# Sums of the attention weights on VectorE for some groups, and other durations in the order's account

## The chip, the cores and the metric

The kernel runs on one core of a Trainium2 chip. The metric is the device time of one execution in microseconds (us), as the median of several runs; a shorter time is better. The engines of the core are TensorE (PE), VectorE (DVE), ScalarE (ACT), GpSimd (POOL) and SyncE (SP), which issues most DMAs.

## The reference

One transformer block with adaptive layer norm, in float32, on `x` of 8 x 1024 x 512, with 16 heads of 32 and a hidden width of 2048:

```python
mod = jax.nn.silu(condition) @ Wada + bada
sh_a, sc_a, gt_a, sh_m, sc_m, gt_m = jnp.split(mod, 6, axis=1)
xm = _layernorm(x, g1, be1) * (1.0 + sc_a[:, None, :]) + sh_a[:, None, :]
x = x + gt_a[:, None, :] * _attention(xm, Wqkv, Wproj, bproj)      # causal softmax
xm = _layernorm(x, g2, be2) * (1.0 + sc_m[:, None, :]) + sh_m[:, None, :]
x = x + gt_m[:, None, :] * (jax.nn.gelu(xm @ W1 + b1, approximate=False) @ W2 + b2)
```

## The kernel before, in words

**Tiling.** The 8 sequences are cut into 16 blocks of 512 tokens: `blocks[n]` is a sequence and its half h. The 16 heads form four groups g of four heads (`HPG = 4`), each with 32 of 128 partitions. The linear parts (`k`, `q`, `v`, `u`, `proj`, `d`) are products of 128x32 weight columns, four side by side in PE's array; most are done by a Strassen scheme (`strassen`, `down`). `matmul` (line 212) issues the four column tiles; in float32 each shows up as two records.

**Attention.** For each group, `scores_at_once` fills the one score tile (`st`, four banks of PSUM) with scores by query, and DVE takes their row maxima (lines 1607 and 1610). `weights_T` fills the same tile with scores by key minus the maxima; ACT takes the exponential into a slot in SBUF (`pT`, line 1698). There are three slots, in `free_p`. POOL masks the diagonal (line 1703). `weigh` multiplies the weights with V into `po`, and `add_weights` lets POOL add every further unit's weights to those of the group's first unit (line 1816), whose slot is the sum, `acc`. The small last unit of groups 0 and 2 is shared with the following group, and its slot is held until both have used it.

**The end of a group** (`finish`, line 1736). Four matmuls with a 128x32 tile of ones add `acc` over its 128 keys and spread the sum over the 32 partitions of each head (line 1747, column-tiled). After them the slot is free. ACT copies the sums into `rec` (line 1756) and `po` into `top` (line 1759); DVE inverts `rec` in four pieces of 128 columns (line 1765); POOL multiplies the two into `qT` (line 1790), which `proj` reads later. Once the end of group 3 is done, `written["attended", n]` lets `proj` of block n go.

**The order.** The program of each engine is written in the order in which Python emits it. An account, `now`, keeps a time for each engine, and `note`, `note_pe` and `note_act` add a duration for each instruction and keep the times at which results are ready (`written`) and buffers free (`left`). PE's part of the account adds `SWITCH` when the tiling changes between "rows" (scores) and "columns" (the rest). Decisions are taken from the account: which thread of linear work goes next (`work`), how much of it is put ahead of an attention unit (`step_aside`), whether a copy goes to DVE or ACT (`sooner`), an addition to DVE or POOL (`either`), or a combination to DVE alone or to an ACT copy and an addition (`combine_out`). Work off PE waits in `jobs`; `run_jobs` emits the head of that list once its operands are due, and `run_jobs(True)` emits all of it.

Of the kernel before, what the change touches and what calls it, by code (L numbers as in the profile page):

```python
# [22 lines left out]
def kernel(  # L23
# [112 lines left out]
    def note_pe(ns, form, reads=(), writes=()):  # L136
        now["PE"] = max(now["PE"], due(reads, writes))
        if shape[0] != form:
            shape[0] = form
            now["PE"] += SWITCH  # L140
        note("PE", ns, reads)
        spent[0] += ns
        for k in writes:
            written[k] = now["PE"] + PIPE
# [14 lines left out]
    def either(out, a, b, op, reads, writes):  # L159

        n = 1
        for d in out.shape[1:]:
            n *= d
        on_dve, on_pool = 60 + 1.24 * n, 120 + 2.28 * n
        t = due(reads, writes)
        if max(now["DVE"], t) + on_dve + margin[0] < max(now["POOL"], t) + on_pool:
            nc.vector.tensor_tensor(out, a, b, op)
            note("DVE", on_dve, reads, writes, port=True)
        else:
            nc.gpsimd.tensor_tensor(out, a, b, op)  # L170
            note("POOL", on_pool, reads, writes)
# [29 lines left out]
    def combine_out(out, bank, src, other, reads=(), writes=(), op=ALU.add, last=True):  # L201
        ready = due([("l", bank)], writes)
        if op is ALU.add and out is not other and max(now["DVE"], ready) > max(now["ACT"], ready) + 3500:
            nc.scalar.copy(out, src)
# [7 lines left out]
    def matmul(ps, lhsT, rhs, start, stop, reads=(), bank=None):  # L212
# [8 lines left out]
        for d in rhs.shape[1:]:  # L221
            n *= d
        note_pe(2 * COLUMN * n, "columns", reads, [] if bank is None else [("l", bank)])

# [383 lines left out]
    def normalize(tiles, key, sources):  # L608
# [31 lines left out]
        def power():  # L640
# [468 lines left out]
    def up(step):  # L1109
        _, n, q = step  # L1110

        def gelu():
            for i in range(NC):
# [4 lines left out]
                k = q // 2 + 1  # L1118
                note_act(590, "gelu", [("h", n, q)], [(n, f"B{k}1"), (n, f"B{k}2"), ("g", n, q)])

# [435 lines left out]
    def scores_by_heads(n, g, parts, reads):  # L1556

        h = blocks[n][1]
        for some in (range(HPG - 1), range(HPG - 1, HPG)):
            step_aside(reads, [BANK])  # L1560
            of = {j: lin_bank() for j in some}
            for qt, kh, c0, w, gg in parts:
                for j, bank in of.items():
# [8 lines left out]
                    )  # L1572
                note_pe(2 * COLUMN * w, "rows", reads, [("l", bank) for bank in of.values()])
            for j, bank in of.items():
# [13 lines left out]
    def scores_at_once(n, g, parts, reads):  # L1588
# [3 lines left out]
        for qt, kh, c0, w, gg in parts:  # L1592
            for j in range(HPG):
# [8 lines left out]
                )  # L1602
            note_pe(2 * COLUMN * w, "rows", reads, ["st"])
        if parts[0][1] == h:
# [10 lines left out]
    def split_maxima(n, g, h):  # L1615
# [47 lines left out]
    def weights_T(n, g, parts):  # L1663
# [18 lines left out]
        for k, c0, w, gg in parts:  # L1682
            kT = keys_of(n, k // NTT)
            for j in range(HPG):
# [51 lines left out]
    def finish(n, g):  # L1736

        run_jobs(True)
        acc, slot = totals.pop((n, g))
        more = unadded if (n, g) == first_end else []  # L1740
        step_aside([("acc", n, g), *(("p", slot) for *_, slot in more)], [BANK])
# [42 lines left out]
        def quotient():  # L1784
# [4 lines left out]
            else:  # L1789
                nc.gpsimd.tensor_tensor(qTs[n][:, g, :], top, rec, ALU.mult)  # L1790
                note("POOL", 1285, [kr, "top"], [("att", n)])
            if g == NC - 1:
                written["attended", n] = 0.0

        for i in range(3):
            add_job(lambda i=i: invert(i), [kr], g == NC - 1)
        add_job(quotient, [kr], g == NC - 1)

    shared = {}

    def add_weights(n, g, parts, pT, slot):
# [5 lines left out]
        for _, c0, w, _ in parts:  # L1807
            for j in range(HPG):
# [6 lines left out]
                else:  # L1815
                    nc.gpsimd.tensor_tensor(into, into, pT[:, j, c0 : c0 + w], ALU.add)  # L1816
                    note("POOL", 230 + 2.07 * w, *keys)

# [175 lines left out]
```

## Time and profile before

| | |
|---|---|
| median of 3 runs | 3510.68 us (3505.79 to 3512.32) |
| profiled execution | 3510.74 us, of which the span is 3509.0 us |
| mean granted TensorE clock | 0.998 |
| HBM | 425.57 MB read, 55.64 MB written |

The profile is of one execution. "Busy" is the time in which an engine has an instruction running; PE's matmuls are pipelined, so that a busy PE is not PE at its peak. PEld is the loading of weights, which overlaps PE. In the groups by line, each row is line, engine, operation, output from inputs, shapes and count, then busy us and the mean ns of one, then the idle time just before them with what ended it. A window row has the busy time of PE, PEld, DVE, ACT and POOL with the instructions in brackets.

### The profile page before, as it was taken

The page shows a single profiled execution, that of the slowest core. Times are in us where ns is not written, and L with a number is a line of the kernel's source. Part 1 is how long each engine was busy: PE and PEld are TensorE (multiplying, and loading weights), DVE is VectorE, ACT ScalarE, POOL GpSimd, SP SyncE. Part 2 cuts the span into 40 slices and gives each one's busy share as a digit, 9 for nine tenths or more (in the row PEclk, how much of TensorE's full clock was granted, in tenths as well). Part 3 has the DMA queues.
Part 4 walks back from the last instruction along what each step waited for, and adds up shares of the span by engine and source line. Part 5 has one row for each costly group of instructions (what it writes and reads, how often), then busy time and mean ns, then how long its engine had stood idle before and what let it go on. Part 6 is the DMA issues. An engine that isn't in the chain of part 4 may idle for free.

```text
span 3509.0 us, 120365 instructions
## 1 busy us (share of the span) xinstructions
PE 3454.3 (98%) x54429; PEld 1724.0 (49%) x54429; DVE 2198.9 (63%) x2401; ACT 1212.4 (35%) x1276; POOL 2084.2 (59%) x2258
## 2 busy tenths in 40 slices
PE   8999999999999999999999999999999999999999
PEld 4444445445554545445454454544555444554445
DVE  5766676564666656665666566765666756656563
ACT  2335333342233423335223342333423343232531
POOL 3767846666366663756727576275753658537660
PEclk9999999999999999999999999999999999999999
DMA  6843444535545445363454534545354544443334
GB/s 212 263 137 104 137 115 140 142 107 159 142 125 156 119 147 153 119 170 115 137 157 130 155 117 144 150 137 148 116 155 137 165 122 146 128 136 101 96 121 140
DMA packets 328194, 491.10 MB, mean 140 GB/s; under 512 B 27260, under 2 KB 177596, under 8 KB 324100
## 3 DMA queue, kind: packets, MB, share of 16 engines
q1 hardware_dynamic: 327568, 483.39, 47.1%
q8 instruction: 428, 7.01, 0.8%
q14 instruction: 82, 0.67, 0.1%
q10 hardware_dynamic: 116, 0.03, 0.0%
HBM read 425.57 MB, written 55.64 MB: 137 GB/s over the span
## 4 chain that ended last, share of the span: by engine, by line
PE 83%; POOL 7%; DMA 3%; DVE 3%; ACT 1%; issue 1%; SPq 1%; ACTq 0%; DVEq 0%; POOLq 0%
PE bank L217 59%; PE sc L1595 8%; PE st L1686 6%; PE po L1726 6%; POOL pT L1816 4%; PE st L1674 2%; PE bank L1747 2%; DMA hat_m<-held_m 1%; DVE mx L1610 1%; POOL hT L170 1%; ACT pT L1698 1%; DMA held_m<-xm_m 1%; PE bank L1648 0%; POOL xr L170 0%; DMA w<-in_L_cond_Wqkv_dram 0%
## 5 line engine op out<-in xcount | busy, mean ns | idle before, releaser
L1816 POOL TENSOR_TENSOR pT<-pT,pT 128x256 f32<-128x256 f32 (+3 forms) x1254 | 1219.7, 1007 | 298.5 <-PE po L1726 181.6
L1698 ACT ACTIVATE pT<-st 128x2048 f32<-128x2048 f32 x288 | 540.9, 1878 | 1065.1 <-PE st L1686 959.8
L217 PE MATMUL bank<-w,hT 128*32 128x256 f32 x14336 | 823.7, 380 | 0.4 <-issue 0.4
L1610 DVE TENSOR_REDUCE mx<-sc 128x4 f32<-128x2048 f32 (+3 forms) x384 | 665.9, 1755 | 235.6 <-PE sc L1595 229.5
L217 PEld LDWEIGHTS bank<-w,hT 128*32 128x32 f32 x14336 | 446.7, 110 | 390.3 <-issue 105.8
L217 PE MATMUL bank<-xm_m,w 128*32 128x256 f32 x8192 | 498.6, 381 | 3.6 <-ACT xm_m L774 2.2
L217 PE MATMUL bank<-t_m,w 128*32 128x256 f32 x6144 | 382.4, 380 | 0.9 <-DVE t_m L786 0.6
L217 PEld LDWEIGHTS bank<-xm_m,w 128*32 128x32 f32 x8192 | 255.6, 110 | 231.2 <-issue 62.2
L1703 POOL TENSOR_SCALAR_AFFINE_SELECT pT<-pT 128x512 f32<-128x512 f32 x256 | 167.5, 672 | 331.9 <-ACT pT L1698 329.4
L1607 DVE TENSOR_TENSOR sc<-sc,mask 128x1024 f32<-128x1024 f32 (+1 forms) x160 | 162.8, 1018 | 293.3 <-PE sc L1595 237.8
L1595 PE MATMUL sc<-kT,qT 32*128 32x512 f32 (+3 forms) x3072 | 329.5, 521 | 4.3 <-ACT pT L1698 3.3
L1726 PE MATMUL po<-pT,v 128*32 128x512 f32 (+3 forms) x3048 | 301.6, 490 | 3.9 <-POOL pT L1703 3.9
L1686 PE MATMUL st<-qT,kT 32*128 32x512 f32 (+3 forms) x3072 | 300.8, 487 | 0.0
L217 PEld LDWEIGHTS bank<-t_m,w 128*32 128x32 f32 x6144 | 189.6, 110 | 172.9 <-issue 48.5
L1765 DVE RECIPROCAL rec<-rec 128x128 f32<-128x128 f32 x256 | 227.3, 922 | 48.2 <-ACT rec L1756 48.2
L217 PE MATMUL bank<-xm_a,w 128*32 128x256 f32 x3968 | 243.4, 382 | 0.4 <-DMA w<-in_L_cond_Wqkv_dram 0.4
L217 PE MATMUL bank<-w,qT 128*32 128x512 f32 x2048 | 237.0, 595 | 1.1 <-DMA w<-in_L_cond_Wproj_dram 0.7
L1595 PEld LDWEIGHTS sc<-kT,qT 32*128 32x128 f32 x3072 | 129.6, 183 | 188.2 <-issue 88.4
L208 DVE TENSOR_TENSOR hT<-bank,u_u 128x512 f32<-128x512 f32 x187 | 126.6, 686 | 105.8 <-PE bank L217 103.1
L217 PE MATMUL bank<-t_a,w 128*32 128x256 f32 x2944 | 183.2, 380 | 0.0
L217 PEld LDWEIGHTS bank<-xm_a,w 128*32 128x32 f32 x3968 | 123.5, 110 | 110.3 <-issue 29.3
L1115 ACT ACTIVATE hT<-hT,cols 128x512 f32<-128x512 f32 x256 | 164.7, 712 | 35.9 <-DVE hT L208 28.5
(243 smaller groups left out, 3404.0 us busy)
## 6 DMA issues: line engine op xcount, KB each, us to landing
w<-in_L_cond_W_dram SPq DMA_DIRECT2D x384, 256.0 KB
w<-kept_up_S SPq DMA_DIRECT2D x256, 256.0 KB
w<-kept_down_S SPq DMA_DIRECT2D x256, 256.0 KB
w<-kept_qkv_S SPq DMA_DIRECT2D x180, 256.0 KB
w<-in_L_cond_Wqkv_dram SPq DMA_DIRECT2D x147, 256.0 KB
hat_a<-in_x_dram SPq DMA_DIRECT2D x64, 256.0 KB
xr<-in_x_dram SPq DMA_DIRECT2D x32, 512.0 KB
w<-in_L_cond_Wproj_dram SPq DMA_DIRECT2D x64, 256.0 KB
```

Of the source, the lines that this page charges most:

```text
L208: nc.vector.tensor_tensor(out, src, other, op)
L217: nc.tensor.matmul(ps[r, :], columns, rhs, start=start, stop=stop, skip_group_check=True)
L1115: nc.scalar.activation(hT[:, i, :], hT[:, i, :], AF.Gelu, bias=cols[:, O_B1 + f : O_B1 + f + 1])
L1595: nc.tensor.matmul(sc[:, j, c0 : c0 + w], qTs[n][r, gg, ts(qt, P)], keys_of(n, kh)[r, gg, :w], start=True, stop=True, skip_group_check=True,)
L1607: nc.vector.tensor_tensor(place, place, shape_of.to_broadcast(place.shape), ALU.add)
L1610: nc.vector.tensor_reduce(maxima[n, gg][:, kh, qt, :], sc[:, :, c0 : c0 + w], axis=AX.X, op=ALU.max)
L1686: nc.tensor.matmul(st[:, j, c0 : c0 + w], kT[r, gg, ts(k % NTT, P)], qT[r, gg, TB - w :], start=False, stop=True, skip_group_check=True,)
L1698: nc.scalar.activation(pT[:, :, :used], st[:, :, :used], AF.Exp, scale=scale)
L1703: nc.gpsimd.affine_select(diagonal, diagonal, pattern=[[0, HPG], [1, P]], compare_op=ALU.is_ge, fill=0.0, base=0, channel_multiplier=-1,)
L1726: nc.tensor.matmul(po[r, TB - w :], v[:, k % NTT, g * P + j * hd : g * P + (j + 1) * hd], pT[:, j, c0 : c0 + w], start=(k == 0), stop=last ...
L1765: nc.vector.reciprocal(some, some)
L1816: nc.gpsimd.tensor_tensor(into, into, pT[:, j, c0 : c0 + w], ALU.add)
```

## The change

At the end of a group of blocks 4 to 14, if DVE's account is less than 1500 ns past PE's, the sum over keys is made in another way (`finish_turned`): DVE transposes the slot in 32x32 squares in place, so that keys lie along the free axis, and adds over them to 128x64 partial sums (`few`); the slot is free then. Four matmuls of 16 columns with `folded`, four identities of 32 stacked over the partitions, add the four partial sums. DVE inverts these 128x16 sums, and a transpose that reads each of them 32 times spreads them over `rec`. The copy of `po`, and POOL's product, are as before. `weights_T` emits all waiting jobs if no slot is free. Apart from that, several durations of the account change, and so does the limit from which `combine_out` uses ACT and an addition.

```diff
@@ note_pe
-            now["PE"] += SWITCH
+            now["PE"] += SWITCH - (36 if form == "rows" else 45)
@@ either
-        on_dve, on_pool = 60 + 1.24 * n, 120 + 2.28 * n
+        on_dve, on_pool = 60 + 1.24 * n, 110 + 2.52 * n
@@ combine_out
-        if op is ALU.add and out is not other and max(now["DVE"], ready) > max(now["ACT"], ready) + 3500:
+        if op is ALU.add and out is not other and max(now["DVE"], ready) > max(now["ACT"], ready) + 500:
@@ matmul
-        note_pe(2 * COLUMN * n, "columns", reads, [] if bank is None else [("l", bank)])
+        note_pe(2 * COLUMN * n + 2, "columns", reads, [] if bank is None else [("l", bank)])
@@ constants
+    folded = const.tile([P, hd], F32, tag="folded", name="folded")
+    for j in range(HPG):
+        nc.gpsimd.tensor_copy(folded[j * hd : (j + 1) * hd, :], ident[j * hd : (j + 1) * hd, j * hd : (j + 1) * hd])
@@ normalize, power
-            note("POOL", 1500, [("mv", key)], [("rstd", key)])
+            note("POOL", 1850, [("mv", key)], [("rstd", key)])
@@ up, gelu
-                note_act(590, "gelu", ...
+                note_act(705, "gelu", ...
@@ scores_by_heads, scores_at_once
-            note_pe(2 * COLUMN * w, "rows", reads, ...
+            note_pe(2 * COLUMN * w + 104, "rows", reads, ...
@@ split_maxima
-                note("POOL", 250, [("mx", n, g)], [("rows", n, g)])
+                note("POOL", 310, [("mx", n, g)], [("rows", n, g)])
@@ weights_T
+        if not free_p:
+            run_jobs(True)
         slot = free_p.pop(0)
@@ finish
         run_jobs(True)
         acc, slot = totals.pop((n, g))
+        if 3 < n < NB - 1 and now["DVE"] < now["PE"] + 1500:
+            finish_turned(n, g, acc, slot)
+            return
@@ quotient
-                note("POOL", 1285, [kr, "top"], [("att", n)])
+                note("POOL", 1340, [kr, "top"], [("att", n)])
@@ add_weights
-                    note("POOL", 230 + 2.07 * w, *keys)
+                    note("POOL", 245 + 2.13 * w, *keys)
@@ new
+    def finish_turned(n, g, acc, slot):
+        top = tmp.tile([P, TB], F32, tag="top", name=f"top_{n}_{g}", bufs=1)
+        rec = tmp.tile([P, TB], F32, tag="rec", name=f"rec_{n}_{g}", bufs=1)
+        nc.scalar.copy(top, outs.pop((n, g)))
+        note_act(585, None, ["po"], ["top"])
+        few = small.tile([P, HPG, HPG * NTT], F32, tag="few", name=f"few_{n}_{g}", bufs=1)
+        inverse = small.tile([P, HPG * NTT], F32, tag="inverse", name=f"inverse_{n}_{g}", bufs=1)
+        turned = acc.rearrange("p j (a i) -> p j a i", i=hd)
+        key = ("few", n, g)
+        written[key] = NEVER
+        def turn_acc():
+            flat = acc.rearrange("p j n -> p (j n)")
+            nc.vector.transpose(flat, flat)
+            note("DVE", 2330, [("acc", n, g), ("p", slot)], [("p", slot)])
+        def sum_acc():
+            nc.vector.tensor_reduce(few, turned, axis=AX.X, op=ALU.add)
+            note("DVE", 2300, [("p", slot)], [key])
+            free_p.append(slot)
+        def spread_sums():
+            yield [key], [BANK]
+            bank = lin_bank()
+            for j in range(HPG):
+                r = slice(j * hd, (j + 1) * hd)
+                nc.tensor.matmul(
+                    banks[bank][r, : HPG * NTT], folded, few[:, j, :],
+                    start=True, stop=True, skip_group_check=True,
+                )
+            note_pe(120, "columns", [key], [("l", bank)])
+            def invert():
+                nc.vector.reciprocal(inverse, banks[bank][:, : HPG * NTT])
+                live[bank] = False
+                note("DVE", 260, [("l", bank)], [("inv", n, g)])
+                spread_out = inverse.unsqueeze(2).to_broadcast([P, HPG * NTT, hd])
+                nc.vector.transpose(rec.rearrange("p (a i) -> p a i", i=hd), spread_out)
+                note("DVE", 700, [("inv", n, g)], ["rec"])
+                nc.gpsimd.tensor_tensor(qTs[n][:, g, :], top, rec, ALU.mult)
+                note("POOL", 1285, ["rec", "top"], [("att", n)])
+                if g == NC - 1:
+                    written["attended", n] = 0.0
+            add_job(invert, [("l", bank)], True)
+        add_job(turn_acc, [("acc", n, g)], True)
+        add_job(sum_acc, [("p", slot)], True)
+        start(spread_sums())
```

More of the change, by code (lines that the diff above doesn't have):

```diff
@@ L1118, in gelu @@
                 k = q // 2 + 1
-                note_act(590, "gelu", [("h", n, q)], [(n, f"B{k}1"), (n, f"B{k}2"), ("g", n, q)])
+                note_act(705, "gelu", [("h", n, q)], [(n, f"B{k}1"), (n, f"B{k}2"), ("g", n, q)])
         def finished():
@@ L1572, in scores_by_heads @@
                     )
-                note_pe(2 * COLUMN * w, "rows", reads, [("l", bank) for bank in of.values()])
+                note_pe(2 * COLUMN * w + 104, "rows", reads, [("l", bank) for bank in of.values()])
             for j, bank in of.items():
@@ L1602, in scores_at_once @@
                 )
-            note_pe(2 * COLUMN * w, "rows", reads, ["st"])
+            note_pe(2 * COLUMN * w + 104, "rows", reads, ["st"])
         if parts[0][1] == h:
```

## The prediction

> **What bounds the kernel now.** I read the page first: busy shares, granted clock, the chain that ended last.
>
> ```profile
> span 3509.0 us, 120365 instructions
> PE 3454.3 (98%) x54429; PEld 1724.0 (49%) x54429; DVE 2198.9 (63%) x2401; ACT 1212.4 (35%) x1276; POOL 2084.2 (59%) x2258
> PE 83%; POOL 7%; DMA 3%; DVE 3%; ACT 1%; issue 1%; SPq 1%; ACTq 0%; DVEq 0%; POOLq 0%
> ```
>
> TensorE (PE) is busy 98% of the span, VectorE (DVE) 63%, GpSimd (POOL) 59%. Shares are averages, so the windows come next. The group ends of blocks 4 to 14, where the edit can act, lie in the second but for the last two (columns: PE, PEld, DVE, ACT, POOL busy, clock, DMA).
>
> ```profile
> 0.00:440.00 440.00, 411.90 (x6537) 205.49 (x6541) 290.45 (x326) 152.36 (x155) 286.74 (x328) 0.99 0.56 170
> 440.00:3080.00 2640.00, 2623.02 (x41298) 1308.37 (x41292) 1668.74 (x1819) 924.35 (x972) 1586.90 (x1731) 1.00 0.48 138
> ```
>
> In those 2640 us PE is idle for 17.0 us, 0.6%, at the full clock. Busy records can hide stretching, so I check the pace of the records in the timeline of PE (start, duration, count):
>
> ```profile
> 2154.84 0.64 PE L1726 MATMUL po<-pT,v 128*32 128x256 f32 x8
> 2155.30 1.04 PE L1747 MATMUL bank<-pT,ones 128*32 128x512 f32 x8
> 2156.16 1.04 PE L217 MATMUL bank<-w,qT 128*32 128x512 f32 x8
> ...
> 2179.07 1.91 PE L217 MATMUL bank<-t_a,w 128*32 128x256 f32 x32
> 2180.80 1.91 PE L217 MATMUL bank<-w,xm_a 128*32 128x256 f32 x32
> 2182.52 1.91 PE L217 MATMUL bank<-w,t_a 128*32 128x256 f32 x32
> 2184.25 1.48 PE L217 MATMUL bank<-w,xm_a 128*32 128x256 f32 x24
> ```
>
> In the last four rows a product of 32 records of 256 columns starts 1.73, 1.72 and 1.73 us after the one before it, 54 ns a record, with no gap. PE streams back to back, and what leaves its stream should leave the span. The Trainium skill's page "Perfetto Trace Analysis", section "Identifying the Most-Contended Engine", says that matmul busy share is no fair measure and wants weight-load busy beside it; that share is 49% here, which would leave PE room. What it would mean for the time is a rival below.
>
> **What the change removes from PE.** At an end that is turned, the four matmuls with ones go (eight records of 512 columns). Those at 2155.30 start 0.86 us before the next thing on PE, and both neighbours use the same column tiling, so no change of form goes with them: 0.86 us off PE.
>
> **What it adds to PE.** Four matmuls with 16 columns each, eight records. Before has no such shape; the nearest has 8 columns and the same 128x32 weights:
>
> ```profile
> 11.98 1.29 PE L217 MATMUL bank<-condT,w 128*32 128x8 f32 x64 [0.35 <-DMA w<-in_L_cond_Wada_dram]
> 13.55 1.15 PE L217 MATMUL bank<-condT,w 128*32 128x8 f32 x64 [0.27 <-DMA w<-in_L_cond_Wada_dram]
> 15.05 0.30 PE L217 MATMUL bank<-condT,w 128*32 128x8 f32 x8 [0.35 <-DMA w<-in_L_cond_Wada_dram]
> ```
>
> 64 records take 1.15 to 1.29 us, 18 to 20 ns each, so eight take 0.15 us inside a stream; eight alone took 0.30 us, most of it the drain of the last, which overlaps the next matmul in a stream. I take 0.15, with 0.30 as the upper end: 0.71 us saved per turned end, at least 0.56. The Trainium skill, "TensorE: Matmul & The Clock Gate", section "Wait — 56ns, not 53.3ns?", has a floor of about 25 ns from start to start however few columns; the 18 ns above are under it. By that floor eight records would take 0.20 us and the saving would be 0.66 us an end.
>
> **How many ends are turned.** The condition is decided while the program is ordered: blocks 4 to 14 (44 ends), and DVE's account less than 1.5 us past PE's. Carrying the kernel's own bookkeeping through with the durations of before, 34 ends pass and 10 don't (in that account DVE is ahead by 1.52, 1.54, 1.57, 1.94, 2.87, 3.33, 3.36, 3.91, 5.39 and 8.61 us). The highest that passes is at 1.16. Three sit just above the limit and the change moves the account, so I keep 28 to 38 and take 34. This is only a count of branches.
>
> 34 x 0.71 = 24.1 us off PE (28 x 0.56 = 15.7 to 38 x 0.71 = 27.0).
>
> **What it does to the other engines.** The groups by line, with shapes kept apart (busy, mean ns of one, idle before):
>
> ```profile
> L1756 ACT COPY rec<-bank 128x512 f32<-128x512 f32 x64 | 37.2, 582 | 123.0 <-PE bank L1747 86.2 <-POOL qT L1790 28.5 <-DVE qT L1787 8.4
> L1765 DVE RECIPROCAL rec<-rec 128x128 f32<-128x128 f32 x256 | 227.3, 922 | 48.2 <-ACT rec L1756 48.2
> L1610 DVE TENSOR_REDUCE mx<-sc 128x4 f32<-128x2048 f32 x192 | 439.8, 2291 | 232.3 <-PE sc L1595 229.5
> L700 DVE STREAM_TRANSPOSE xm_a<-hat_a 128x512 f32<-128x512 f32 x56 | 35.1, 674 | 0.0
> L1816 POOL TENSOR_TENSOR pT<-pT,pT 128x512 f32<-128x512 f32 x504 | 662.0, 1346 | 209.5 <-ACT pT L1698 114.5 <-PE po L1726 92.7
> L1790 POOL TENSOR_TENSOR qT<-top,rec 128x512 f32<-128x512 f32 x61 | 79.8, 1308 | 123.7 <-DVE rec L1765 123.6
> ```
>
> ACT loses one copy, 0.58 us. DVE loses four reciprocals, 4 x 0.92 = 3.69 us, and gains a transpose of 2048 columns, a sum over 2048, a reciprocal of 16 columns and a transpose of 512. The sum is priced by the maxima's reduce, 2.29; the long transpose lies between that and four short ones, 4 x 0.674 = 2.70 (the diff books 2.33, which I take); the short transpose is 0.67; the small reciprocal lies between nothing and the 0.92 of 128 columns (0.26 booked). Together 5.6 us, so DVE gains 1.9 us an end, 34 x 1.9 = 65 us on 1669 busy of 2640: from 63% to 66%. That is not a new bound.
>
> The new sequence is no longer than the old. From the finished sum of weights to the quotient it was 0.86 + 0.58 + 3.69 + 1.31 = 6.4 us; it becomes 2.33 + 2.29 + 0.15 + 0.26 + 0.67 + 1.31 = 7.0. The output projection waits for the last of four such ends and has other columns to run meanwhile.
>
> Two things do get later. The slot of weights in SBUF was free after PE's 0.86 us; now it is free after DVE's 4.6. Behind that on DVE stand the maxima of the scores, and behind those, PE's next user of the only score tile. A bank of PSUM that ACT emptied in 0.58 us is now held until DVE has inverted; PE has three such banks. An end with the rows around it:
>
> ```profile
> 2119.54 0.82 PE L1747 MATMUL bank<-pT,ones 128*32 128x512 f32 x4
> ...
> 2121.57 1.23 DVE L1607 TENSOR_TENSOR sc<-sc,mask 128x1024 f32<-128x1024 f32 x1 [1.95 <-PE sc L1595]
> ...
> 2122.84 2.36 DVE L1610 TENSOR_REDUCE mx<-sc 128x4 f32<-128x1536 f32 x2
> ...
> 2125.81 0.12 PEld L1674 LDWEIGHTS <-minus_ones 32*128 32x128 bf16 x8 [0.41 <-DVE xm_a L784]
> ...
> 2127.30 1.88 ACT L1698 ACTIVATE pT<-st 128x2048 f32<-128x2048 f32 x1 [3.01 <-PE st L1686]
> ```
>
> DVE is free for 1.95 us at this end and gets 4.6 us of work, so mask and maxima move back by up to 2.7 us and the weights of 2125.81 with them. PE loses nothing as long as the order puts a projection there instead, and the account knows the new durations. What DVE costs PE today is small (waits of PE in the middle window: total, times, longest):
>
> ```profile
> PE st L1674 <- DVE mx L1610: 3.0, 6, 0.7
> ...
> PE bank L217 <- DVE t_m L786: 0.6, 1, 0.6
> ...
> PE bank L1648 <- DVE hT L208: 0.4, 1, 0.4
> ```
>
> That is 4.0 us. DVE's share rises by a twentieth, but in long pieces, so I let these waits double: +4.0 us.
>
> **The edited durations and the limit of 500.** They reorder the program from the start. The new values lie nearer to the trace:
>
> ```profile
> L1115 ACT ACTIVATE hT<-hT,cols 128x512 f32<-128x512 f32 x256 | 164.7, 712 | 35.9 <-DVE hT L208 28.5 <-POOL hT L170 6.7
> L170 POOL TENSOR_TENSOR hT<-hT,hT 128x1024 f32<-128x1024 f32 x29 | 78.2, 2714 | 16.1 <-DVE hT L1212 16.1
> ...
> L204 ACT COPY hT<-bank x5: 585/586/588, 293.7 to 3270.1; 128x512 f32<-128x512 f32 x5
> ...
> L204 ACT COPY u_u<-bank x1: 587/587/587, 234.1 to 234.1; 128x512 f32<-128x512 f32 x1
> ```
>
> A gelu took 712 ns (booked 590, then 705); a 1024-column POOL operation 2714 (booked 2455, then 2690); an addition of weights 1346 (1290, then 1336). The lower limit sends more combinations to an ACT copy and an addition: today there are 20 at L204 in seven rows, of which the first and last stand here. Each more takes about 0.69 us off DVE and puts 0.58 on ACT and some 1.3 on POOL; a hundred more would bring POOL to 63%, still cover. The worth of a better order is at most the 17.0 us of idle time; a worse one can cost as much. I take zero and keep half of it, 8.5 us, for the range. The four small copies of `folded` cost nothing: POOL waits 16.9 us for weights right after its constants.
>
> ```profile
> POOL sums_k L826 <- DMA w<-in_L_cond_Wqkv_dram: 16.9, 1, 16.9
> ```
>
> **Sum.** The profiled execution took 3510.74 us (span 3509.0 and 1.7 around it), and the median of the three runs is 3510.68, so no correction is needed. 3510.7 - 24.1 + 4.0 = 3490.6 us.
>
> **Rivals.**
> (a) *The slot is late, slower.* After ends of groups 0 and 2 in a block the unit that straddles two groups still holds the third slot, so the next exponential can only take the slot that is being turned. Of the 34 ends, 19 are such. If POOL's additions or DVE's queue run later than booked, the exponential waits, the score tile stays full, and PE, which runs in order, stands before the next scores or weights. With one of the two long DVE operations uncovered, 2.3 us, it is 19 x 2.3 = 43.7 us: 3510.7 - 24.1 + 43.7 = 3530.3. It decides from 24.1 / 19 = 1.3 us an end. For it: the 1.95 us of room against 4.6 above. Against it: PE's waits on DVE are never longer than 0.7 us today, and PE has projections to run. Chance 0.15.
> (b) *The new order is worse, slower.* Repricing brings back stalls that the present order has not: twice the 17.0 us of idle time against 24.1 gives 3510.7 - 24.1 + 34 = 3520.6. For it: every decision in the program may move. Against it: the new prices fit the rows better. Chance 0.09.
> (c) *No change.* PE is not the bound after all, as the 49% would have it, or few ends pass the condition and the saving is eaten: 3510.7. The even 1.73 us per product speak against it. Chance 0.12.
> (d) *More than forecast.* 38 ends and half of the idle time gone: 3510.7 - 27.0 - 8.5 = 3475.2. Chance 0.08.
>
> **Numbers.** The forecast's own case has 0.56, with a range of its own from 3478 to 3503 (27.0 saved and a few us of waits gone; 15.7 saved and 8.5 of waits more). A difference under 0.2%, 7 us, is about what measurement can't tell from none. Faster: 0.56 + 0.08 = 0.64, same 0.12, slower 0.15 + 0.09 = 0.24. The range reaches from (d), 3475, to 3518, short of (b) and (a), whose heavier halves are left out.
>
> **What would show it.** Right: in the changed profile the ones matmuls count 536 - 34 x 8 = 264 records, a DVE transpose and a reduce over 2048 columns appear some 34 times at about 2.3 us, PE busy falls by about 24 us, and PE's idle time in the middle stays near 20 us. Wrong by (a): PE or ACT's exponentials wait for the new sums in DVE, in the list of waits. Wrong by (b): idle time grows at lines that have nothing to do with the turned ends, before block 4 too. Wrong by (c): PE busy falls and the span doesn't.

## The result: 15 us slower

| | before | after |
|---|---|---|
| median | 3508.76 us (6 runs, 3505.79 to 3512.32) | 3523.59 us (6 runs, 3516.64 to 3524.26) |
| profiled execution | 3510.74 us, span 3509.0 | 3523.91 us, span 3522.2 |
| mean granted clock | 0.998 | 0.995 |

The ratio of the times is 1.0037 [1.0024, 1.005]: slower, by more than the 0.2% below which the prediction takes a difference for none. The forecast was 3490.6 us, and the range ended at 3518.

The page after, its first lines and the chain that ended last:

```profile
span 3522.2 us, 120545 instructions
PE 3437.7 (98%) x54429; PEld 1724.0 (49%) x54429; DVE 2286.7 (65%) x2368; ACT 1299.3 (37%) x1431; POOL 2207.7 (63%) x2305
PE 79%; DVE 7%; DMA 5%; POOL 4%; ACT 3%; issue 2%; SPq 1%; ACTq 0%; DVEq 0%; POOLq 0%
```

TensorE (PE) is busy for 16.6 us less than the 3454.3 of before, and yet the span is 13.2 us longer: the time in which PE is idle (span less busy) went from 54.7 to 84.5 us. The groups of the new operations, shapes kept apart:

```profile
L1821 DVE STREAM_TRANSPOSE pT<-pT 128x2048 f32<-128x2048 f32 x30 | 69.0, 2301 | 0.6 <-POOL pT L1875 0.6
L1825 DVE TENSOR_REDUCE few<-pT 128x64 f32<-128x2048 f32 x30 | 68.4, 2279 | 0.4
L1755 PE MATMUL bank<-pT,ones 128*32 128x512 f32 x272 | 38.2, 593 | 0.4 <-DVE b_gate_m L208 0.4
L1845 DVE STREAM_TRANSPOSE rec<-inverse 128x512 f32<-128x512 f32 x30 | 21.3, 711 | 1.2
L1841 DVE RECIPROCAL inverse<-bank 128x16 f32<-128x16 f32 x30 | 7.5, 250 | 16.3 <-PE bank L1834 15.4 <-ACT pT L1703 1.0
L1834 PE MATMUL bank<-few,folded 128*32 128x16 f32 x240 | 7.1, 184 | 0.0
```

30 ends are turned, with 240 small records. Four pieces on VectorE (DVE) take 2.30 + 2.28 + 0.25 + 0.71 = 5.54 us an end. The small matmuls hold PE's stream for less than their duration, because the next product overlaps them:

```profile
894.06 0.22 PE L1834 MATMUL bank<-few,folded 128*32 128x16 f32 x8
894.12 1.04 PE L217 MATMUL bank<-xm_a,w 128*32 128x256 f32 x16
```

The next start is 0.06 us behind theirs, and 0.05 to 0.09 us at all 30 ends. Now the windows (PE, PEld, DVE, ACT, POOL busy, clock, DMA):

```profile
0.00:440.00 440.00, 410.25 (x6497) 206.70 (x6497) 286.00 (x322) 167.06 (x184) 295.15 (x319) 0.98 0.56 173
440.00:3080.00 2640.00, 2596.55 (x41085) 1296.14 (x41089) 1745.84 (x1784) 986.93 (x1085) 1692.87 (x1780) 1.00 0.47 137
```

In the middle window PE's idle time is 43.5 us (2640 less 2596.55), where it was 17.0. One more loss hides in "busy": where the granted clock is below full, records take longer. Over the 350 windows of 10 us up to 3500, the sum of (1 - clock) x 10 us is 6.8 us before and 15.3 after. So the work taken off PE is reckoned at 16.6 + 8.5 = 25.1 us, or 0.84 an end: -25.1 of work, +29.8 of idle time and +8.5 of clock make the +13.2 us. The work is what is left over in this sum, not measured by itself. The rows bear its size out: the ones start 0.86 us before the next matmul, the small records 0.06, which makes 0.80 an end. So the turned ends take off PE what was forecast or a little more; 38.3 us come back in other ways.

The list of waits of PE in the middle window says where (total, times, longest):

```profile
PE st L1677 <- DVE mx L1613: 11.3, 9, 3.2
PE bank L217 <- ACT p_v L197: 8.3, 4, 2.9
PE sc L1598 <- ACT pT L1703: 5.3, 9, 1.0
PE bank L217 <- ACT p_k L197: 3.5, 2, 2.2
PE bank L217 <- ACT p_q L197: 1.7, 1, 1.7
...
PE bank L217 <- ACT p_d L197: 1.2, 1, 1.2
PE bank L1651 <- DVE mcols L1635: 1.2, 3, 0.5
PE bank L217 <- DVE hT L1215: 1.1, 2, 0.6
PE sc L1598 <- DVE mx L1613: 1.0, 3, 0.5
...
PE bank L217 <- DVE t_a L789: 0.7, 1, 0.7
```

Waits that DVE ends make 15.3 us, where they made 4.0. Waits that ACT ends make 24.6 us in all, of which the copies `p_v`, `p_k`, `p_q` and `p_d` are 14.7. The same view of before has 5.6 us ended by ACT, and of these copies only one row:

```profile
PE bank L217 <- ACT p_v L197: 0.5, 1, 0.5
```

No row of these lists of PE names a turned sum. ACT's list over the span does:

```profile
ACT pT L1703 <- DVE few L1825: 33.3, 9, 4.2
```

Nine exponentials wait for the slot that is being turned. PE waited directly behind five of them, for 0.33 to 0.40 us each, 1.9 us in all, so little of it reached PE. Copies of first products at line 197 come from the linear work, and how one gets late is seen in the timeline (start, duration):

```profile
1280.04 0.56 ACT L204 COPY y_d<-bank 128x512 f32<-128x512 f32 x1
1280.94 1.77 POOL L170 TENSOR_TENSOR t_a<-t_a,xm_a 128x512 f32<-128x512 f32 x1 [2.93 <-DVE t_a L789]
1282.67 1.26 POOL L170 TENSOR_TENSOR y_d<-y_d,u_d 128x512 f32<-128x512 f32 x1
1283.97 0.59 ACT L197 COPY p_v<-bank 128x512 f32<-128x512 f32 x1 [3.37 <-POOL y_d L170]
1284.61 5.35 PE L217 MATMUL bank<-w,xm_a 128*32 128x256 f32 x64 [2.73 <-ACT p_v L197]
```

This is the limit of 500 at work in one place. A combination (`combine_out`) that one DVE operation would have done is now an ACT copy at line 204 and an addition on GpSimd (POOL). Here that addition also reads `u_d`, which lies in the single buffer `p1`. POOL's program stands before `t_a`, which waits for DVE; the addition comes 2 us later; until it has read `p1`, ACT can't copy the next first product, `p_v`, into it; until ACT has, PE's bank is full. PE waits 2.73 us. At five of these waits, 10.3 of the 14.7 us, ACT's copy waits for the addition `y_d<-y_d,u_d`. The rows at line 204 were 20 copies before; now they are 212 in fourteen rows.

The same 64 records of `p_v`'s successor in the trace before:

```profile
1274.26 3.66 PE L217 MATMUL bank<-w,xm_a 128*32 128x256 f32 x64 [0.47 <-ACT p_v L197]
```

They took 3.66 us then and 5.35 now. The wait of 2.73 us was followed by records that took 1.69 us longer, and the windows show the slower clock:

```profile
1280.00:1290.00 10.00, 7.27 (x106) 3.83 (x102) 4.36 (x5) 1.77 (x4) 8.82 (x6) 0.83 0.42 135
1286.00:1286.50 0.50, 0.50 (x8) 0.22 (x4) 0.50 (x1) 0.00 (x0) 0.50 (x1) 0.50 0.00 0
1289.00:1289.50 0.50, 0.50 (x16) 0.30 (x12) 0.00 (x0) 0.00 (x0) 0.50 (x1) 1.00 0.42 102
```

In windows of half a us the clock stands at 0.50 from 1285.5 to 1288.5 and at 1.00 before 1285.0 and after 1289.0. That is a stretch of some 3.4 us at half the clock, a loss of 1.7 us. 6.8 and 15.3 are four and nine times that loss: the clock costs by whole stretches. Of the nine in the changed kernel, seven begin before 450 us or after 3370; in the blocks between, the one at 1284.61 is one of two.

The Trainium skill, "TensorE: Matmul & The Clock Gate", section "What's actually happening", has the clock halved after an idle window of some 3.4 us. By that rule a wait of 2.73 us would cost no clock; the granted clock of 0.50 behind it and the 1.69 us say otherwise, and the measurement decides.

### The profile page after: what moved, and what is told of

It is laid out like the page before. It is cut to its first block, busy times and chain, and to the rows that moved or that the text cites. A ratio compares the mean times of both kernels' runs of the same rounds, so it can differ in the third digit from the quotient of the medians.

```text
span 3522.2 us, 120545 instructions
## 1 busy us (share of the span) xinstructions
PE 3437.7 (98%) x54429; PEld 1724.0 (49%) x54429; DVE 2286.7 (65%) x2368; ACT 1299.3 (37%) x1431; POOL 2207.7 (63%) x2305
## 4 chain that ended last, share of the span: by engine, by line
PE 79%; DVE 7%; DMA 5%; POOL 4%; ACT 3%; issue 2%; SPq 1%; ACTq 0%; DVEq 0%; POOLq 0%
PE bank L217 56%; PE sc L1598 8%; PE st L1689 6%; PE po L1731 6%; PE st L1677 2%; DVE mx L1613 2%; POOL pT L1875 2%; DMA hat_m<-held_m 1%; DMA hat_a<-held_a 1%; PE bank L1755 1%; ACT pT L1703 1%; DVE sc L1610 1%; DMA held_m<-xm_m 1%; DVE xr L167 1%; ACT xm_m L777 1%
## 5 line engine op out<-in xcount | busy, mean ns | idle before, releaser
L1875 POOL TENSOR_TENSOR pT<-pT,pT 128x256 f32<-128x256 f32 (+3 forms) x1254 | 1244.3, 1027 | 212.4 <-PE po L1731 115.5
L1708 POOL TENSOR_SCALAR_AFFINE_SELECT pT<-pT 128x512 f32<-128x512 f32 x256 | 175.7, 704 | 248.8 <-ACT pT L1703 248.6
L208 DVE TENSOR_TENSOR hT<-bank,u_u 128x512 f32<-128x512 f32 x138 | 95.1, 689 | 126.9 <-PE bank L217 118.3
L1689 PEld LDWEIGHTS st<-qT,kT 32*128 32x128 f32 x3072 | 144.5, 187 | 25.8 <-issue 1.5
```

Of the source, the lines that this page charges most:

```text
L208: nc.vector.tensor_tensor(out, src, other, op)
L1689: nc.tensor.matmul(st[:, j, c0 : c0 + w], kT[r, gg, ts(k % NTT, P)], qT[r, gg, TB - w :], start=False, stop=True, skip_group_check=True,)
L1708: nc.gpsimd.affine_select(diagonal, diagonal, pattern=[[0, HPG], [1, P]], compare_op=ALU.is_ge, fill=0.0, base=0, channel_multiplier=-1,)
```

## The experiments

The theory after reading the result: the turned ends save what they should, and the edited durations and the limit make an order in which PE waits. The rival: the turned ends themselves cost the time, through DVE's queue and the slots.

### Which part of the change costs

The change falls into three parts that can be compiled alone: the turned ends (T), the limit of 500 (L) and the durations (P).

```diff
# T off (in L, P, and P with L); folded and the check of free_p stay
-        if 3 < n < NB - 1 and now["DVE"] < now["PE"] + 1500:
+        if False:
# L off
-  ... max(now["ACT"], ready) + 500:
+  ... max(now["ACT"], ready) + 3500:
# P off: every edited duration back, e.g.
-            now["PE"] += SWITCH - (36 if form == "rows" else 45)
+            now["PE"] += SWITCH
```

T alone: 

> The turned ends alone, with the old prices in the account and the old limit of 3500; 35 ends are turned. Theory 'turned ends' (the long DVE pieces make PE wait for the maxima and eat the saving): 3515 to 3530 us, with PE's waits for the maxima at 15 us or more. Theories 'limit' and 'prices' (the loss comes from the other edits): 35 x 0.71 = 25 us under before, about 3484. Theory 'scatter' (any new order of the program comes out some 10 us better or worse): 3474 to 3500.

L alone: 

> The limit of combine_out at 500 alone. Theory 'limit' (ACT, in order, gets to the first products' copies late, and PE waits for the bank): 3515 to 3530 us, with PE waiting for the ACT copies of p_k, p_q, p_v by 10 us or more. Theories 'turned ends' and 'prices': as before, 3506 to 3512. Theory 'scatter': 3499 to 3525 without a common kind of wait.

P alone: 

> The edited durations of the account alone. Theory 'prices': 3515 to 3530 us, with new waits before block 4 too. Theories 'turned ends' and 'limit': 3500 to 3510. Theory 'scatter': 3499 to 3525.

T and P: 

> All of the change but the limit, which stays at 3500; 33 ends are turned. Theory 'limit': 33 x 0.71 = 23 us under before, about 3485. Theory 'turned ends': 3515 to 3525. Theory 'prices': 3495 to 3515. Theory 'scatter': 3475 to 3505.

P and L: 

> The durations and the limit of 500 without the turned ends. If the turned ends of the changed kernel save 0.71 us each (30 of them, 21 us) and the rest costs: 3540 to 3550 us. If the costs of the durations (32 us) and of the limit (34 us) add up: 3565 to 3580. If the turned ends are what makes the changed kernel slower: 3505 to 3515.

T and L: 

> All of the change but the edited durations; 35 ends turned. If the turned ends gain against the limit alone (3542) as they do against the durations alone (22 us): 3520. If the durations are what costs: 3500 or less. If every new order is a draw of its own, without a sum over the edits: anywhere in 3500 to 3545.

P was cut once more. One half has PE's durations only (`SWITCH`, + 2, + 104), the other has those of POOL and of the gelu only:

```diff
# PE's half keeps
+            now["PE"] += SWITCH - (36 if form == "rows" else 45)
+        note_pe(2 * COLUMN * n + 2, ...
+            note_pe(2 * COLUMN * w + 104, "rows", ...
# the other half keeps
+        on_dve, on_pool = 60 + 1.24 * n, 110 + 2.52 * n
+                note_act(705, "gelu", ...      # and POOL's 1850, 310, 1340, 245 + 2.13 * w
```

PE's half: 

> Of the edited durations only those of TensorE: a smaller SWITCH, 104 ns more for scores, 2 ns more for a product. If the scores' higher price makes the account hold TensorE's own work for later than it is, and so emits VectorE's and ACT's work late: 3525 to 3545. If GpSimd's and ACT's prices are what costs: 3505 to 3515. If any new order is a draw: anywhere in 3505 to 3540.

The other half: 

> Of the edited durations only those of GpSimd and ACT (additions, roots, small copies, gelu). If they are what costs: 3525 to 3545. If TensorE's prices are: 3505 to 3515. If any new order is a draw: anywhere in 3505 to 3540.

And two kernels measure what an order without any better or worse knowledge costs: before, with the duration of a PE column changed in its last digit.

```diff
-    COLUMN = 0.84
+    COLUMN = 0.841      # the other kernel: 0.839
```

0.841: 

> Before with one constant of the account, COLUMN, at 0.841 instead of 0.84: a difference without meaning, that puts 39% of TensorE's matmuls at another place. Theory 'any other order costs' (the order of before is a good draw): 3525 to 3545 us, as with the limit alone and the durations alone. Theory 'the edits themselves are bad': as before, 3505 to 3512.

0.839: 

> The same with COLUMN at 0.839; 35% of the matmuls at another place. Theory 'any other order costs': 3525 to 3545 us. Theory 'the edits themselves are bad': 3505 to 3512.

Measured (each ratio is to executions of before taken beside it; the last three columns are of the profiled execution, in us; idle is its span less PE busy, and the clock loss is reckoned as above; the profiled execution of 0.839 took 3518.8 us, less than the median, and that of T 3521.5, more):

| kernel | median us | ratio to before | PE busy | PE idle | clock loss |
|---|---|---|---|---|---|
| before | | 1 | 3454.3 | 54.7 | 6.8 |
| T | 3513.90 | 1.0017 [1.0008, 1.0025] | 3432.2 | 87.6 | 15.3 |
| L | 3542.04 | 1.0094 [1.0081, 1.0107] | 3465.5 | 73.1 | 13.6 |
| P | 3540.10 | 1.0083 [1.0069, 1.0097] | 3460.3 | 79.3 | 13.6 |
| P, PE's half | 3527.45 | 1.0061 [1.0048, 1.0073] | 3460.3 | 68.9 | 15.4 |
| P, other half | 3524.64 | 1.0052 [1.0038, 1.0066] | 3458.0 | 64.2 | 10.2 |
| P and L | 3531.09 | 1.0072 [1.0058, 1.0085] | 3459.0 | 70.6 | 10.2 |
| T and P | 3517.73 | 1.0027 [1.0019, 1.0036] | 3430.7 | 87.7 | 10.2 |
| T and L | 3511.24 | 1.0007 [0.9998, 1.0015] | 3434.8 | 73.9 | 13.6 |
| T, P and L (after) | 3523.59 | 1.0037 [1.0024, 1.005] | 3437.7 | 84.5 | 15.3 |
| before, 0.841 | 3510.66 | 1.0007 [0.9998, 1.0016] | 3453.8 | 55.1 | 6.8 |
| before, 0.839 | 3525.95 | 1.0049 [1.0037, 1.0062] | 3453.9 | 63.2 | 1.7 |

Few of the ranges were met. T came out just under its range for costly turned ends and far above the 3484 of the other theories, L and P above every range, P and L between two of them. T and P, T and L, the halves of P and the neutral kernels fell into one of theirs, but no theory has them all.

Without one turned end, P and L cost 0.72%, 25 us of 3510. In that trace DVE's busy time is 2228.8 us, little above the 2198.9 of before, and the middle window loses PE time all the same:

```profile
440.00:3080.00 2640.00, 2607.96 (x40939) 1294.49 (x40935) 1682.67 (x1779) 992.00 (x1099) 1694.74 (x1775) 1.00 0.47 137
```

32.0 us idle instead of 17.0, and its list of waits has the maxima, at 8.0 us, first again:

```profile
PE st L1677 <- DVE mx L1613: 8.0, 7, 3.2
PE sc L1598 <- ACT pT L1703: 5.6, 5, 1.7
...
PE bank L217 <- ACT p_v L197: 2.3, 2, 1.5
```

So most of the longer waits for DVE (15.3 us after, 13.7 here) need no turned sums. They come with a new order. L alone has 9.3 us of them, P alone 15.2. Waits for the copies `p_v` to `p_d` come with a new order too: P alone, with the limit at 3500, has 6.6 us, P and L with 500 only 4.3.

T alone makes a new order as well, with 47.9 us of PE idle in the middle window. Its largest row there, and what ACT stood for at the longest of its waits:

```profile
PE bank L217 <- ACT xm_m L777: 8.3, 3, 6.0
```

```profile
1362.06 2.22 ACT L777 ACTIVATE xm_m<-hat_m,shiftm,gainm 128x512 f32<-128x512 f32 x3 [12.47 <-DMA hat_m<-held_m]
```

ACT waits for a transfer of the linear work, and again no row of PE's waits names a turned sum.

The turned ends are worth different amounts on different orders: 0.87% (31 us) on L, 0.56% (20 us) on P, 0.35% (12 us) on P and L, and alone, where they still move the rest of the program, they cost 0.17%, where the forecast's own terms for them, 24.1 saved and 4.0 of waits, make a gain of 0.57%. The share of each edit depends on the order in which they are added: T first, then P and L, is +0.17% and +0.20%; P and L first, then T, is +0.72% and -0.35%. The parts don't add up: L costs 0.94%, P 0.83%, the two together 0.72%. A last digit of `COLUMN`, which says nothing new to the account, makes 0.07%, which can't be told from nothing, or 0.49%. That L, P and both halves of P each cost something on the order of before is shown; on top of T, L costs nothing. Why each does is open, and so is how much of it is due to what the new durations say and how much to reordering as such: two neutral kernels are too few for that.

### The buffer p1

If the chain of the timeline above costs what it seems to, after with its own order kept to the instruction, but with the 48 combinations that read `p1` done by one DVE operation, should get most of `p_v`'s and `p_k`'s waits back. The account keeps its entries, so that nothing moves:

```diff
+            alone_on_dve = "p1" in reads and not (max(now["DVE"], ready) > max(now["ACT"], ready) + 3500)
+            if not alone_on_dve:
                 nc.scalar.copy(out, src)
...
-            either(out, out, other, op, [*reads, *writes], writes)
+            either(out, out, other, op, [*reads, *writes], writes, not alone_on_dve)   # books only
+            if alone_on_dve:
+                nc.vector.tensor_tensor(out, src, other, op)
```

> The changed kernel with its order kept, but 48 combinations that read the first product's buffer (p1), which the limit of 500 sends to an ACT copy and a GpSimd or VectorE addition, are one VectorE operation again. Theory 'limit: the late addition holds the p1 buffer, and the next first product's copy and with it TensorE waits': the waits for ACT's p_v, p_k, p_q, p_d, 14.7 us in the changed kernel, fall under 5 us, and the time by 8 to 15 us, to 3508 to 3516. Rival 'TensorE would wait for something else there': 3520 to 3526.

Measured: 3512.48 us, 1.0006 [0.9998, 1.0015], 11 us under after. PE idle 78.0 us, clock loss 5.1 instead of 15.3. The list of waits of PE:

```profile
PE st L1683 <- DVE mx L1619: 15.8, 11, 3.8
...
PE bank L223 <- ACT p_v L199: 2.9, 3, 1.3
...
PE bank L223 <- ACT p_k L199: 2.5, 2, 1.5
```

`p_v` fell from 8.3 to 2.9 us, and its longest wait from 2.9 to 1.3. With `p_k`, `p_q` (1.4) and `p_d` (1.2) the waits for first products are 8.0 us, where they were 14.7; the 5 us that were expected are missed, the time is in the range. The idle time fell by 6.5 us, just these waits. The profiled clock loss fell by 10.2 us, but that is not all `p1`: of the six stretches fewer only the one behind 1284.61 follows a wait for a first product, and a wait of 2.41 us for the maxima, at 708.93 in after, is here too, without a stretch behind it. Over all executions the granted clock is 0.9963 after and 0.9970 here on average, which makes some 2 us. So 11 us by the medians is what the edit gave; about 7 us of it are waits, and the rest is assigned only in part, to the clock. The edit also takes 48 copies off ACT and some 40 us off POOL, which isn't separated from the buffer. The maxima stay: 17.1 us over the whole span of after, 15.8 here.

A version of after with its limit at 3500 where `p1` is read, and only the ends of odd groups turned, with an order of its own:

```diff
-  ... max(now["ACT"], ready) + 500:
+  ... max(now["ACT"], ready) + (3500 if "p1" in reads else 500):
-        if 3 < n < NB - 1 and now["DVE"] < now["PE"] + 1500:
+        if g % 2 and 3 < n < NB - 1 and now["DVE"] < now["PE"] + 1500:
```

> The changed kernel with two repairs in its own account: the limit of 500 doesn't hold where the p1 buffer is read, and only ends of groups 1 and 3 are turned, after which another slot is free. If both mechanisms are what costs, and the order is no worse a draw than the others: 3495 to 3508. If new orders cost 20 to 30 us whatever their edits: 3510 to 3530.

Measured: 3510.95 us, 1.0009 [1.0, 1.0018]; PE busy 3442.6, idle 66.9. Fewer ends turned and no wait on `p1` by the limit give the time of before, no better than after with `p1` alone, and above the range for the two mechanisms.

### Turned ends in the order of before

To separate the new operations from the new order, the next kernels keep the order of before on every engine. The account is fed the old durations and the old decisions; at 38 ends the long transpose and the sum stand where the four matmuls with ones were emitted, and the small matmuls, the inversion and the product come 8 us later by the account.

```diff
+            nc.vector.transpose(flat, flat)
+            nc.vector.tensor_reduce(few, ..., axis=AX.X, op=ALU.add)
+            late.append((now["PE"] + 8000, spread))   # spread: folded, inverse, rec, product
             # bank for folded: of the free ones, the last emptied
```

> The order of before kept on every engine, decisions and account alike; only at 38 group ends the turned operations are put in the place of the old ones, and the four small matmuls, the inversion and the product 8 us later in PE's account. Theory 'turned ends save, any other order costs': 38 x 0.71 = 27 us less TensorE work, some of it given to waits for VectorE: 3480 to 3492 us. Theory 'turned ends do not pay' (VectorE's long pieces eat the saving in any order): 3505 to 3520.

Measured: 3585.08 us, 1.0215 [1.0201, 1.0229], at a clock of 0.991 and 133 us of PE idle. Both theories are missed by far. This is rival (a) of the prediction, at larger size. Its timeline, and two rows of its waits of PE:

```profile
1074.31 1.14 PE L1610 MATMUL sc<-kT,qT 32*128 32x512 f32 x8
1074.62 2.30 DVE L1777 STREAM_TRANSPOSE pT<-pT 128x2048 f32<-128x2048 f32 x1
1076.96 2.29 DVE L1778 TENSOR_REDUCE few<-pT 128x64 f32<-128x2048 f32 x1
...
1079.98 2.26 DVE L1625 TENSOR_REDUCE mx<-sc 128x4 f32<-128x2048 f32 x1
...
1082.29 2.09 PE L1610 MATMUL sc<-kT,qT 32*128 32x512 f32 x8 [4.11 <-DVE mx L1625]
```

```profile
PE st L1689 <- DVE mx L1625: 32.8, 17, 4.2
...
PE sc L1610 <- DVE mx L1625: 20.8, 14, 4.1
```

The two long pieces hold DVE for 4.6 us, the maxima come after them, and PE's next scores stand for 4.11 us. 53.6 us in two rows. So DVE has the room on average and not at the place.

The same with short pieces, to price their length: transpose and sum over 256 of the 2048 columns, and an addition in place of the inversion. Seven eighths of the sum are left out.

```diff
-            nc.vector.transpose(flat, flat)
+            nc.vector.transpose(flat[:, :256], flat[:, :256])
-                nc.vector.reciprocal(inverse, ...)
+                nc.vector.tensor_scalar(inverse, ..., 1.0, None, ALU.add)
```

> The kept order with 38 turned ends again, but the transpose and the sum on VectorE run over 256 instead of 2048 columns each (seven eighths of the sum is left out, and the inversion is an addition of one). TensorE's work is the same as in the kept order with full sums. Theory 'the long pieces on VectorE make TensorE wait, and the waits slow its clock': the waits for the maxima fall back to some 10 us, the clock to 0.998, and the saved TensorE work shows: 3508 - 38 x 0.86 = 3475, so 3470 to 3485 us. Rival 'the small matmuls stand at a bad place of TensorE's queue': above 3540.

Measured: 3528.75 us, 1.0049 [1.0036, 1.0062]: 56 us less, between the two ranges. The length of the pieces is most of the cost. But the kernel is still slower than before, with PE busy for 3437.3 us and idle for 91, 36 more than before, which length doesn't explain. PE waited 24.0 us ahead of the small matmuls, for a bank:

```profile
L1783 PE MATMUL bank<-few,folded 128*32 128x16 f32 x304 | 9.3, 188 | 24.0 <-DVE y L208 10.0 <-DVE u_k L208 5.0 <-DVE hT L208 3.6
```

Was the bank badly chosen? Two more kernels take the bank that was emptied first:

```diff
-            late.pop(0)[1](max(free, key=lambda i: left.get(("l", i), 0.0)))
+            late.pop(0)[1](min(free, key=lambda i: left.get(("l", i), 0.0)))
```

Long pieces: 

> The kept order with 38 turned ends and full sums as before, but the small matmuls take the free bank that was emptied first, not last. If the waits for that bank were 24 us and their clock some 10: 3545 to 3560. If the small matmuls wait for VectorE's sums anyway: 3575 to 3590.

Short pieces: 

> The same with the transpose and the sum over 256 columns only (seven eighths of the sum left out, the inversion an addition of one). Theory 'PE-bound: saved work is saved time once nothing new is waited for': 3508 - 38 x 0.86 = 3475, with waits of 5 us more 3475 to 3488. Rival 'PE loses it again elsewhere': 3500 or more.

Measured: 3584.46 us, 1.0219 [1.0205, 1.0233], and 3521.43 us, 1.0041 [1.0028, 1.0053]: not much different, and above the ranges in which the bank or the saved work decides. The wait only moved, as the short version's waits and timeline show:

```profile
PE bank L217 <- DVE inverse L1787: 24.9, 14, 5.3
```

```profile
1304.35 0.23 PE L1783 MATMUL bank<-few,folded 128*32 128x16 f32 x8
1304.88 2.35 DVE L1625 TENSOR_REDUCE mx<-sc 128x4 f32<-128x1024 f32 x2
...
1307.75 0.16 DVE L1787 TENSOR_SCALAR inverse<-bank 128x16 f32<-128x16 f32 x1
1307.96 3.21 PE L217 MATMUL bank<-xm_a,w 128*32 128x256 f32 x32 [3.38 <-DVE inverse L1787]
```

The small matmuls are over in 0.23 us, and their bank is held for 3.3 us more, because the one operation that empties it, 0.16 us long, stands in DVE's queue behind the maxima. PE's next product needs that bank. That is the second cost of moving the inversion's input from an ACT copy to DVE.

The last pair in this order turns only the 23 ends whose slot isn't the next exponential's, emits the two long pieces in the places of the first and third reciprocals, and the small matmuls after them:

```diff
+            pieces.append((slot, lambda: nc.vector.transpose(flat, flat)))
+            pieces.append((slot, lambda: nc.vector.tensor_reduce(few, ...)))
...
+            elif i in (0, 2) and pieces:
+                pieces.pop(0)[1]()
+                    late.append((max(now["PE"], now["DVE"]) + 1500, spread))
```

Bank emptied last: 

> The order of before kept, with full sums, but only at 23 ends whose slot is not the next exponential's, and with the transpose and the sum at the places of the first and third reciprocal, where VectorE is due to be idle. Theory 'the place of the long pieces decides': 23 x 0.86 = 20 us saved, less some 5 us of waits: 3488 to 3500 us. Theory 'turned ends do not pay wherever they stand': 3508 or more.

Bank emptied first: 

> 23 ends, pieces in place of reciprocals, with the bank emptied first. Some 5 us of waits for the bank and a dip of the clock should go: 3496 to 3502. If the bank didn't matter here: 3504 to 3508.

Measured: 3506.15 us, 0.9988 [0.998, 0.9996], and 3503.44 us, 0.999 [0.9981, 0.9999]. The first lies between its two ranges, the second just under that for a bank that doesn't matter. They are the fastest kernels here, 0.1% under before, which is less than the 0.2% of the prediction. The second one's busy times and waits of PE:

```profile
PE 3435.8 (98%) x54429; PEld 1719.4 (49%) x54429; DVE 2242.7 (64%) x2401; ACT 1200.8 (34%) x1253; POOL 2085.2 (60%) x2262
```

```profile
PE bank L217 <- DVE inverse L1790: 9.7, 7, 2.2
PE st L1689 <- DVE mx L1625: 7.3, 8, 2.4
```

PE busy is 18.5 us less than before; with a clock loss of 5.1 us the work is 16.8 less, or 0.73 an end. The maxima cost 7.3 us, where before has 7.8 over its span, and the bank held by DVE's inversion costs 9.7. The span, 3501.0, is 8.0 us shorter: 18.5 of busy time less 10.5 of new idle time, and that bank is the largest row of the waits.

## Why the prediction was wrong

**The step that failed** is "I take zero and keep half of it, 8.5 us, for the range", the term for the edited durations and the limit. They cost 25 us by themselves (P and L, 1.0072). Its bound rested on two errors. "The worth of a better order is at most the 17.0 us of idle time" is true of gains. The next half sentence, that a worse one can cost as much, is not a bound: the loss has no ceiling at the idle time of today. And that the new durations lie nearer to the trace was used as a reason for a good order. Not all do: the product at the end of a group took 1308 ns, booked 1285 before and 1340 now. P alone costs 0.83%.

The same zero is missing for the turned ends. They change the account too, and T alone, without P and L, is 0.17% slower where 0.57% faster was forecast. So the forecast priced no new order at all, whichever edit made it. Which property of an order makes it slow stays open.

Rival (b) names this mechanism, at a chance of 0.09, and its 3520.6 is close to the 3523.6 measured. The closeness is in part luck: its doubled idle time had no measured price, and 8.5 us of the rise are clock. Of its two signs, one held, idle time at lines that have nothing to do with turned ends (line 197). The other didn't: the first 440 us have 29.8 us of idle time, 28.1 before.

**"Each more takes about 0.69 us off DVE and puts 0.58 on ACT and some 1.3 on POOL ... still cover"** had POOL's busy share right (63%), with 192 more copies where a hundred were supposed, and missed what the addition holds while it waits in POOL's queue. `p1` is one buffer, and 48 such additions read it. Taking them back gave 11 us, about 7 of them in named waits.

**Work off PE** was a little larger an end than the 0.71 us forecast: 0.73 in the order of before, 0.84 by the sum after, 0.80 by the rows. The small records hold the stream for 0.06 us, not 0.15. 30 ends were turned instead of 34, so the total, 25.1 us against 24.1, is right by two errors that cancel.

**"I let these waits double: +4.0 us."** In the middle window the waits for DVE went from 4.0 to 15.3, +11.3. 13.7 us are there without turned ends, so a new order is enough to make them, and the term had the wrong cause besides the wrong size. Turned ends on top of P and L gained 12 us, against 20.1 by the sum.

**The clock** had no term. It cost 8.5 us in the profiled executions, and no step asked what a wait does to the records behind it.

**"The new sequence is no longer than the old"** contradicts its own figures, 6.4 and 7.0 us: it is 0.6 us longer. What that costs isn't measured by itself. The bank held for DVE, which the prediction names without a term, costs 9.7 us in the last kernel in the order of before; no wait of PE names it in the changed kernel.

**Rival (a)**, the slot or DVE's queue late, had half of its sign: ACT's exponentials wait 33.3 us for the new sums. But PE stood behind them for 1.9 us only, and no wait of PE names the sums, so it is not what slowed the changed kernel. In the order of before it happens, and dearer than 43.7 us: 3585.1 us with 38 ends, against 3513.9 for T alone, whose order is made with the new pieces in the account.

**Rival (c)**: the Trainium skill's "Perfetto Trace Analysis", section "Identifying the Most-Contended Engine", judges PE's room by weight-load busy together with the share of peak arithmetic, which was not worked out here; weight loading alone, at 49%, would not call PE the bound. The rival's sign, that PE busy falls and the span doesn't, is there in the changed kernel, but so are 29.8 us of new idle time on PE, so it doesn't decide. In the last kernel 18.5 us less of PE busy time came with 10.5 us of new idle time and a span 8.0 us shorter, 0.1% by the medians. That fits a bound by PE and is too small to settle it.

**Costs on DVE** were right: 2.30, 2.28, 0.25 and 0.71 us measured, 5.54 an end against 5.6.

## What to carry to other kernels

In a kernel whose order is computed from booked durations, an edit of those durations is an edit of the whole order. Price it by measurement, alone, before anything is summed with it; here such edits cost from nothing that can be told (0.07%) to 0.94%, where 25 us taken off TensorE are 0.7%. An edit of the operations that enters the account is one too. When work is moved to an engine with room, ask which single buffer or bank it holds while it stands in that engine's queue, and who needs that next: the busy share doesn't show it.

## What was not expected of the hardware

A wait of PE can cost more than its length. After 2.73 us of waiting, 64 records took 5.35 us instead of 3.66, at half the clock for some 3.4 us. Not each such wait does it: in the same trace a wait of 2.41 us (at 708.93) had such a stretch behind it, and waits of 2.21 (1535.19) and 2.86 us (1720.51) had none. What decides is open. In the order of before with long pieces, the wait of 4.11 us lies in this window:

```profile
1080.00:1090.00 10.00, 7.71 (x68) 2.95 (x68) 6.09 (x7) 0.00 (x0) 0.00 (x0) 0.66 0.60 130
```

At 0.66 it is 3.4 us by the same reckoning as above, two stretches. A part of that fell into the wait itself, which lasted to 1082.29 while the clock stood at 0.50 from 1081.5 on; the rest came on top, and the eight records of scores behind the wait took 2.09 us where the eight at 1074.31 took 1.14. The total of idle time doesn't set this loss: after with `p1` read by DVE has 78.0 us of idle time and 5.1 of clock loss, T and L have 73.9 and 13.6.
